# Experts' gate and up projections in three parts of 128 columns instead of four of 96

## The chip, the cores and the metric

The kernel runs on one core of one Trainium2 chip. The metric is the device time of one execution in microseconds (us). The core has a matrix engine (TensorE, PE in the profile; its weight loads have a row of their own, PEld), a vector engine (VectorE, DVE), a scalar engine (ScalarE, ACT), a general engine (GpSimd, POOL) and a sync engine (SyncE, SP) that issues most of the transfers. The 16 DMA engines of the core are shared by all queues. All data is fp32.

## The reference

The input is 16 sequences of 512 tokens with 256 features, 8192 tokens in all. Four layers follow one another, each with a layer norm ahead of it and a residual around it: a softmax attention, a mixture of experts, a forgetting linear attention, and the same mixture of experts again, with the same weights. Only the mixture of experts is touched here:

```python
logits = x @ router_w.T                          # 64 experts
topk_w, topk_ids = top_k(softmax(logits), 8)     # weights scaled to sum 1
# every expert takes at most C = 128 tokens, in order of the tokens
g = einsum('ecd,edf->ecf', xb, w_gate)           # 256 -> 192
u = einsum('ecd,edf->ecf', xb, w_up)             # 256 -> 192
h = silu(g) * u
y = einsum('ecf,efd->ecd', h, w_down)            # 192 -> 256
routed = sum over a token's experts of weight * y
gu = x @ ws_gate_up                              # shared expert, 256 -> 384
shared = silu(gu[:, :192]) * gu[:, 192:] @ ws_down
return routed + shared
```

## The kernel before

`hybrid_block_kernel` calls `attention`, `experts`, `forget_attention`, `experts` and `joined` in this order. `experts` (line 822) runs twice and has two phases, both ordered by hand on TensorE, VectorE, ScalarE and GpSimd (`manual_schedule`, line 1170): an engine executes in the order in which the code issues. The transfers that SP issues are placed among each other by a planner with its own costs, and SP takes them strictly in that order.

**Dense phase** (lines 1188 to 1203). It goes over 16 blocks of 512 tokens. In step `b` the code issues, in this order: `load(b+4)`, `normed(b+2)` (layer norm, line 97), `features(b+1)` (eight transposes of the normed block, line 910, and two copies by ScalarE, line 913), `shared(b-3)` (the shared expert's gate and up, line 989), `logits(b+1)` (line 919), `choose(b)` (the eight best experts, VectorE, lines 941 to 955), `likely(b+1)` (lines 931 to 936), `count(b-1)` (running counts of the tokens of each expert: a transpose, line 968, a copy, line 970, a scan, line 973, and two transfers through DRAM, lines 978 and 979), `down(b-4)` (the shared expert's down projection, line 1007, with copies at line 1014) and `moments(b+3)` (line 71). All PSUM results come from one pool of eight banks that are handed out in turn; one step takes two for `features`, four for `shared`, and one each for `logits`, `count` and two for `down`. A bank that is asked for waits until its last user eight banks earlier has been read.

**Shared expert.** `shared` (line 984) makes the 384 columns of gate and up in four parts of 96: two of gate, two of up, each in its own PSUM bank, 96 partitions x 512 tokens, with two matmuls over the 256 inputs. An fp32 matmul is two TensorE instructions in the profile, each with its own weight load, so a block has 16 at line 989. Then `gated` (line 813) is called twice. It computes silu(g) * u as 0.5 * (tanh(g/2) + 1) * g * u: one tanh on ScalarE (line 817) and two VectorE instructions (lines 818 and 819), the second waiting for the first.

**Expert loop** (lines 1204 to 1212). It goes over the 64 experts. In step `e`: `gather(e+6)` fetches the tokens of an expert by an indirect transfer that POOL issues (line 1108); a piece of `find` places the tokens of later experts (lines 1034 to 1083); `turned(e+2)` transposes the gathered tokens (line 1119) and copies them (VectorE, line 1121); `widened(e+1)` makes gate and up in four parts of 96 columns (line 1132: 16 TensorE instructions, 128 tokens each, all into one PSUM bank) and calls `gated` on 96 x 256 elements; `narrowed(e)` makes the down projection with two halves of 96 rows (line 1147: 4 instructions), scales it on ScalarE (line 1155) and adds it into DRAM by an indirect transfer that POOL issues (line 1158). Even and odd experts add into different tensors; a scatter into a tensor waits until the one before it into the same tensor has landed. `fetch` (line 1089) loads the weights of two experts with three transfers of 384 KB (gate, up, down) on SP; four such pairs fit (`p4`), so pair k+4 can be loaded when pair k has been used: the gate tile after line 1132 has read it, the down tile after line 1147 has.

Of the kernel before, what the change touches and what calls it, by code (L numbers as in the profile page):

```python
# [9 lines left out]
F32 = mybir.dt.float32  # L10
# [20 lines left out]
FP = 96  # L31
# [5 lines left out]
class Block:  # L37
# [775 lines left out]
    def gated(self, out, gate, up, pool, half):  # L813

        nc = self.nc
        th = pool.tile(list(out.shape), F32, name="th")
        nc.scalar.activation(th, gate, AF.Tanh, scale=0.5)  # L817
        nc.vector.scalar_tensor_tensor(th, th, 1.0, gate, ALU.add, ALU.mult)  # L818
        nc.vector.scalar_tensor_tensor(out, th, half, up, ALU.mult, ALU.mult)  # L819


    def experts(self, x, y, weights):
# [7 lines left out]
        with ExitStack() as c:  # L830
# [10 lines left out]
            nc.sync.dma_start(out=rw_sb, in_=rw.rearrange("(k p) f -> p k f", p=P))  # L841
            wsg_sb = w.tile([P, KD, 2 * FF], F32, name="wsg_sb")
            nc.sync.dma_start(out=wsg_sb, in_=ws_gu.rearrange("(k p) f -> p k f", p=P))
            wsd_sb = w.tile([FP, 2, D], F32, name="wsd_sb")
            nc.sync.dma_start(out=wsd_sb, in_=ws_down.rearrange("(k p) f -> p k f", p=FP))

# [32 lines left out]
            def bank():  # L879
                return pb.tile([P, BLK], F32, name="pb")  # L880
# [103 lines left out]
            def shared(b):  # L984
                xnT = xnTs.pop(b)
                gu = [bank() for m in range(4)]
                for m in range(4):
                    for kd in range(KD):
                        nc.tensor.matmul(  # L989
                            gu[m][0:FP, :],  # L990
                            lhsT=wsg_sb[:, kd, ts(m, FP)],
                            rhs=xnT[:, kd, :],
                            start=(kd == 0),
                            stop=(kd == KD - 1),
                        )
                hT = hTs[b] = p2.tile([FP, 2, BLK], F32, name="hT")
                for m in range(2):
                    self.gated(hT[:, m, :], gu[m][0:FP, :], gu[2 + m][0:FP, :], p2, 0.5)

            def down(b):  # L1000
                hT = hTs.pop(b)
                out = p2.tile([P, CB, D], F32, name="y")
                for i in range(0, CB, 2):
                    py = bank()
                    for k in range(2):
                        for m in range(2):
                            nc.tensor.matmul(
                                py[:, ts(k, D)],
                                lhsT=hT[:, m, ts(i + k, P)],
                                rhs=wsd_sb[:, m, :],  # L1010
                                start=(m == 0),
                                stop=(m == 1),
                            )
                    nc.scalar.copy(
                        out[:, i : i + 2, :], py.rearrange("p (c d) -> p c d", c=2)
                    )
                nc.sync.dma_start(
                    out=y[ts(b, BLK), :].rearrange("(c p) d -> p c d", p=P), in_=out
                )
# [66 lines left out]
            xes, xeTs, hes, ws = {}, {}, {}, {}  # L1086
            accs = (x, y)

            def fetch(e):

                es = slice(e, e + 2)
                wg = p4.tile([P, 2, KD, FF], F32, name="wg")
                nc.sync.dma_start(
                    out=wg, in_=w_gate[es].rearrange("e (p k) f -> p e k f", k=KD)
                )
                wu = p4.tile([P, 2, KD, FF], F32, name="wu")
                nc.sync.dma_start(
                    out=wu, in_=w_up[es].rearrange("e (p k) f -> p e k f", k=KD)
                )
                wd = p4.tile([FP, 2, 2, D], F32, name="wd")  # L1100
                nc.sync.dma_start(
                    out=wd, in_=w_down[es].rearrange("e (k p) f -> p e k f", p=FP)
                )
                ws[e // 2] = (wg, wu, wd)
# [19 lines left out]

            def widened(e):
                wg, wu, _ = ws[e // 2]
                xeT = xeTs.pop(e)
                gu = bank()[0:FP, :].rearrange("p (m t) -> p m t", m=4)
                for m in range(4):
                    wm = (wg, wu)[m // 2]  # L1130
                    for kd in range(KD):
                        nc.tensor.matmul(  # L1132
                            gu[:, m, :],
                            lhsT=wm[:, e % 2, kd, ts(m % 2, FP)],
# [4 lines left out]
                hes[e] = p3.tile([FP, 2, CAP], F32, name="he")  # L1139
                self.gated(hes[e], gu[:, 0:2, :], gu[:, 2:4, :], p3, 0.5)  # L1140

            def narrowed(e):
                wd = ws[e // 2][2]
                he = hes.pop(e)
                py = bank()
                for m in range(2):
                    nc.tensor.matmul(  # L1147
                        py[:, 0:D],
                        lhsT=he[:, m, :],
                        rhs=wd[:, e % 2, m, :],  # L1150
                        start=(m == 0),
                        stop=(m == 1),
                    )
# [16 lines left out]
            with tc.manual_schedule(  # L1170
# [34 lines left out]
                for e in range(-ahead, E):  # L1205
                    run(e + ahead, E, gather)
                    place((e + 14) // many * many, 1)
                    run(e + 2, E, turned)
                    run(e + 1, E, widened)
# [141 lines left out]
```

## Time and profile before

| | |
|---|---|
| three runs | 2975.1, 2981.86, 2982.6 us |
| median | 2981.86 us |
| the profiled execution | 2975.03 us, span 2972.9 us, mean granted TensorE clock 0.942 |
| attention | about 0 to 1299 us |
| first `experts`: dense phase, then expert loop | 1299 to 1598 us, 1598 to 1823 us |
| forgetting attention | about 1823 to 2376 us |
| second `experts` | 2376 to 2895 us |
| `joined` | to the end |

A window row gives for each engine its busy time and its number of instructions, then the granted clock of TensorE (1.00 is full speed), the share of the 16 DMA engines that was busy, and GB/s. A timeline row gives start, length, engine, line, operation, tiles and shapes; the square bracket gives the idle time of the engine before it and what ended it. Matmul lengths overlap: the spacing of their starts is what one costs. The stages' limits differ, so each is read from its own window.

### The profile page before, as it was taken

How to read it: one execution, taken by the hardware profiler on the slowest of the kernel's cores; microseconds unless marked ns; L12 is line 12 of the kernel's file. 1: busy time of each engine (PE TensorE's matmuls, PEld its weight loads, DVE VectorE, ACT ScalarE, POOL GpSimd, SP SyncE). 2: the span in 40 equal slices, each digit the busy share in tenths (PEclk: the TensorE clock that was granted, in tenths of full speed). 3: DMA queues.
4: the chain of work that ended last, by engine and by line, in shares of the span. 5: the costliest groups of instructions: out<-in, count | busy, mean ns of one | idle time of the engine just before them, and what ended most of it. 6: DMA issues, size and time to landing. Idle time of an engine off the chain costs nothing. (4 is left out here: it accounts for less than half of the span.)

```text
span 2972.9 us, 49634 instructions
## 1 busy us (share of the span) xinstructions
PE 2709.1 (91%) x19268; PEld 1667.1 (56%) x19268; DVE 1951.1 (66%) x4738; ACT 1153.6 (39%) x2227; POOL 724.9 (24%) x677
## 2 busy tenths in 40 slices
PE   7999999999999999978979995999999879979980
PEld 4444444444444444445648884576666655559870
DVE  5666666666666666537755553999999767736531
ACT  2555655555555565532221221434334212212220
POOL 2000000000000000001104776323322011117773
PEclk8999999999999999879989997999999969989995
DMA  1000000000000000045535996111110164339988
GB/s 44 1 16 16 16 16 16 15 9 8 16 16 16 16 16 8 8 134 135 141 88 158 249 251 156 35 47 53 53 40 27 29 198 133 108 81 246 249 192 339
DMA packets 216649, 252.15 MB, mean 85 GB/s; under 512 B 31712, under 2 KB 206432, under 8 KB 213344
## 3 DMA queue, kind: packets, MB, share of 16 engines
q1 hardware_dynamic: 190688, 202.83, 22.9%
q0 software_dynamic: 24576, 37.77, 6.5%
q10 hardware_dynamic: 1152, 8.39, 0.7%
q8 instruction: 153, 2.51, 0.3%
q14 instruction: 80, 0.66, 0.1%
HBM read 163.67 MB, written 84.74 MB: 84 GB/s over the span
## 5 line engine op out<-in xcount | busy, mean ns | idle before, releaser
L299 DVE TENSOR_REDUCE mx<-sc 128x1 f32<-128x512 f32 x1024 | 635.2, 682 | 395.2 <-PE sc L285 391.6
L326 ACT ACTIVATE pT<-sc 128x512 f32<-128x512 f32 x1024 | 528.7, 603 | 280.6 <-PE sc L285 280.4
L285 PE MATMUL sc<-kT,qT 16*128 16x512 f32 x2048 | 358.9, 611 | 1.4 <-DVE mx L299 1.4
L285 PE MATMUL sc<-qT,kT 17*128 17x512 f32 x2048 | 310.7, 647 | 0.0
L246 POOL TENSOR_TENSOR pad<-t,t 128x512 f32<-128x512 f32 x64 | 81.1, 1267 | 729.5 <-PE sc L285 577.7
L989 PE MATMUL pb<-xnT,wsg_sb 128*96 128x512 f32 x512 | 236.0, 608 | 18.2 <-DVE pr L933 18.2
L285 PEld LDWEIGHTS sc<-kT,qT 16*128 16x128 f32 x2048 | 167.6, 188 | 136.9 <-issue 58.5
L336 PE MATMUL sc<-pT,v 128*32 128x512 f32 x2048 | 241.4, 613 | 0.0
L687 DVE SCALAR_TENSOR_TENSOR pT<-sc,of,left 128x256 f32<-128x256 f32 x512 | 205.8, 473 | 10.3 <-PE sc L670 10.1
L817 ACT ACTIVATE th<-pb 96x256 f32<-96x256 f32 (+1 forms) x192 | 84.0, 453 | 305.5 <-PE pb L1132 266.0
L818 DVE SCALAR_TENSOR_TENSOR th<-th,pb 96x256 f32<-96x256 f32 (+1 forms) x192 | 96.7, 504 | 153.7 <-ACT th L817 152.2
L79 POOL TENSOR_SCALAR va<-mv 128x4 f32<-128x4 f32 x64 | 14.7, 229 | 680.3 <-DVE mv L73 456.4
L646 PE MATMUL pb<-feat,wqk_sb 128*128 128x512 f32 x384 | 176.6, 596 | 1.0 <-DVE left L629 1.0
L285 PEld LDWEIGHTS sc<-qT,kT 17*128 17x128 f32 x2048 | 89.9, 185 | 140.3 <-issue 103.9
L989 PEld LDWEIGHTS pb<-xnT,wsg_sb 128*96 128x96 f32 x512 | 82.5, 167 | 148.6 <-issue 105.2
L1108 POOL DMA_INDIRECT xe<-rows,token x128 | 133.1, 1040 | 111.5 <-DVE token L1082 73.1
L336 PEld LDWEIGHTS sc<-pT,v 128*32 128x32 f32 x2048 | 61.5, 112 | 173.1 <-issue 122.2
L219 PE MATMUL sc<-wqkv_sb,feat 128*128 128x512 f32 x256 | 135.2, 655 | 0.1
L936 ACT ACTIVATE pr<-pr 128x256 f32<-128x256 f32 x32 | 13.3, 417 | 312.5 <-DVE pr L933 308.2
L1132 PE MATMUL pb<-xeT,wg 128*96 128x128 f32 x1024 | 132.9, 273 | 0.4 <-DVE xeT L1121 0.4
L1147 PE MATMUL pb<-wd,he 96*128 96x256 f32 x512 | 131.9, 379 | 1.2 <-DVE he L819 1.2
L1132 PE MATMUL pb<-xeT,wu 128*96 128x128 f32 x1024 | 132.7, 273 | 0.0
(156 smaller groups left out, 4626.2 us busy)
## 6 DMA issues: line engine op xcount, KB each, us to landing
wg<-in_w_gate SPq DMA_DIRECT2D x64, 384.0 KB
wu<-in_w_up SPq DMA_DIRECT2D x64, 384.0 KB
wd<-in_w_down SPq DMA_DIRECT2D x64, 384.0 KB
rows<-xn SPq DMA_DIRECT2D x32, 512.0 KB
routed<-y SPq DMA_DIRECT2D x32, 512.0 KB
x<-in_x SPq DMA_DIRECT2D x16, 512.0 KB
attended<-x SPq DMA_DIRECT2D x16, 512.0 KB
x<-attended SPq DMA_DIRECT2D x16, 512.0 KB
```

The source lines that it names most:

```text
L219: nc.tensor.matmul(pq, lhsT=xnTs[b][:, kd, ts(i, P)], rhs=wqkv_sb[:, kd, 0 : 2 * D], start=(kd == 0), stop=(kd == KD - 1),)
L285: nc.tensor.matmul(scs[j], lhsT=lhs[at : at + high, ts(i, P)], rhs=rhs[at : at + high, :], start=True, stop=True,)
L299: nc.vector.tensor_reduce(mxs[n][:, i, j : j + 1], sc, AX.X, ALU.max, negate=True)
L326: nc.scalar.activation(pT[:, j, :], sc, AF.Exp, scale=float(HD) ** -0.5)
L336: nc.tensor.matmul(pav[ts(j, HP), :], lhsT=vs[b % 2][:, i, 4 * hg + j, :], rhs=pT[:, j, :], start=(i == 0), stop=(i == CB - 1),)
L646: nc.tensor.matmul(pq, lhsT=wqk_sb[:, kd, ts(m, P)], rhs=xnTs[b][:, kd, :], start=(kd == 0), stop=(kd == KD - 1),)
L687: nc.vector.scalar_tensor_tensor(pTs[n][:, :, ts(s8, HD)], sc[:, :, ts(s8, HD)], of[:, s8 : s8 + 1], here, ALU.mult, ALU.mult,)
L818: nc.vector.scalar_tensor_tensor(th, th, 1.0, gate, ALU.add, ALU.mult)
L989: nc.tensor.matmul(gu[m][0:FP, :], lhsT=wsg_sb[:, kd, ts(m, FP)], rhs=xnT[:, kd, :], start=(kd == 0), stop=(kd == KD - 1),)
L1108: nc.gpsimd.indirect_dma_start(out=xes[e], out_offset=None, in_=rows, in_offset=bass.IndirectOffsetOnAxis(ap=token[:, e : e + 1], axis=0),)
L1132: nc.tensor.matmul(gu[:, m, :], lhsT=wm[:, e % 2, kd, ts(m % 2, FP)], rhs=xeT[:, kd, :], start=(kd == 0), stop=(kd == KD - 1),)
L1147: nc.tensor.matmul(py[:, 0:D], lhsT=he[:, m, :], rhs=wd[:, e % 2, m, :], start=(m == 0), stop=(m == 1),)
```

## The change

The 192 + 192 columns of gate and up are cut into three parts of 128 instead of four of 96: the first 128 columns of gate, the first 128 of up, and a part that holds the last 64 of gate on partitions 0 to 63 and the last 64 of up on partitions 64 to 127. This applies to the shared expert and to the 64 experts.

For the shared expert the combined part is made when its weights are loaded: the one transfer of `ws_gate_up` becomes three column ranges, and that of `ws_down` becomes two row ranges (128 and 64). For the 64 experts gate and up of a pair share one tile, `wide`, loaded by two transfers as before, and a new ScalarE copy, `joined`, puts the two times 64 columns of one expert side by side in a tile `wc`, one expert earlier than `widened` uses it. `w_down` of a pair is loaded by two transfers, of 128 and of 64 rows. The down projection uses 128 and 64 rows.

`gated` is gone. The tanh and the first VectorE instruction go over 128 partitions, up columns included, whose results are not used; the last multiplication is two VectorE instructions, the second of 64 partitions with its PSUM operand read from partitions 64 to 127. In `shared` the two first VectorE instructions come ahead of the two last ones.

```diff
-FP = 96
+FT = FF - P
...
             wsg_sb = w.tile([P, KD, 2 * FF], F32, name="wsg_sb")
-            nc.sync.dma_start(out=wsg_sb, in_=ws_gu.rearrange("(k p) f -> p k f", p=P))
-            wsd_sb = w.tile([FP, 2, D], F32, name="wsd_sb")
-            nc.sync.dma_start(out=wsd_sb, in_=ws_down.rearrange("(k p) f -> p k f", p=FP))
+            for to, of, n in ((0, 0, FF), (FF, FF + P, FT), (2 * P, FF, P)):
+                nc.sync.dma_start(
+                    out=wsg_sb[:, :, to : to + n],
+                    in_=ws_gu[:, of : of + n].rearrange("(k p) f -> p k f", p=P),
+                )
+            wsd_sb = w.tile([P, 2, D], F32, name="wsd_sb")
+            nc.sync.dma_start(out=wsd_sb[:, 0, :], in_=ws_down[0:P, :])
+            nc.sync.dma_start(out=wsd_sb[0:FT, 1, :], in_=ws_down[P:FF, :])
...
             def shared(b):
                 xnT = xnTs.pop(b)
-                gu = [bank() for m in range(4)]
-                for m in range(4):
+                gu = [bank() for m in range(3)]
+                for m in range(3):
                     for kd in range(KD):
                         nc.tensor.matmul(
-                            gu[m][0:FP, :],
-                            lhsT=wsg_sb[:, kd, ts(m, FP)],
+                            gu[m],
+                            lhsT=wsg_sb[:, kd, ts(m, P)],
...
-                hT = hTs[b] = p2.tile([FP, 2, BLK], F32, name="hT")
+                hT = hTs[b] = p2.tile([P, 2, BLK], F32, name="hT")
+                th = p2.tile([P, 2, BLK], F32, name="th")
                 for m in range(2):
-                    self.gated(hT[:, m, :], gu[m][0:FP, :], gu[2 + m][0:FP, :], p2, 0.5)
+                    nc.scalar.activation(th[:, m], gu[m], AF.Tanh, scale=0.5)
+                    nc.vector.scalar_tensor_tensor(
+                        th[:, m], th[:, m], 1.0, gu[m], ALU.add, ALU.mult
+                    )
+                for o, g, u in (
+                    (hT[:, 0], th[:, 0], gu[2]),
+                    (hT[0:FT, 1], th[0:FT, 1], gu[1][FT:P]),
+                ):
+                    nc.vector.scalar_tensor_tensor(o, g, 0.5, u, ALU.mult, ALU.mult)
...
             def fetch(e):
...
+                wide = p4.tile([P, 2, 2, KD, FF], F32, name="wide")
+                for u, wt in enumerate((w_gate, w_up)):
+                    nc.sync.dma_start(
+                        out=wide[:, :, u], in_=wt[es].rearrange("e (p k) f -> p e k f", k=KD)
+                    )
+                wd = p4.tile([P, 2, 2, D], F32, name="wd")
+                for m, rs in enumerate((slice(0, P), slice(P, FF))):
+                    nc.sync.dma_start(
+                        out=wd[0 : rs.stop - rs.start, :, m, :],
+                        in_=w_down[es, rs].rearrange("e p f -> p e f"),
+                    )
+                ws[e // 2] = (wide, wd)
...
+            def joined(e):
+
+                wc = wcs[e] = p3.tile([P, KD, 2, FT], F32, name="wc")
+                nc.scalar.copy(
+                    wc, ws[e // 2][0][:, e % 2, :, :, P:FF].rearrange("p u k f -> p k u f")
+                )
+
             def widened(e):
-                wg, wu, _ = ws[e // 2]
+                wide = ws[e // 2][0][:, e % 2]
+                wc = wcs.pop(e).rearrange("p k u f -> p k (u f)")
+                parts = (wide[:, 0, :, 0:P], wc, wide[:, 1, :, 0:P])
                 xeT = xeTs.pop(e)
-                gu = bank()[0:FP, :].rearrange("p (m t) -> p m t", m=4)
-                for m in range(4):
-                    wm = (wg, wu)[m // 2]
+                gu = bank()[:, 0 : 3 * CAP].rearrange("p (m t) -> p m t", m=3)
+                for m, part in enumerate(parts):
                     for kd in range(KD):
                         nc.tensor.matmul(
                             gu[:, m, :],
-                            lhsT=wm[:, e % 2, kd, ts(m % 2, FP)],
+                            lhsT=part[:, kd, :],
                             rhs=xeT[:, kd, :],
...
-                hes[e] = p3.tile([FP, 2, CAP], F32, name="he")
-                self.gated(hes[e], gu[:, 0:2, :], gu[:, 2:4, :], p3, 0.5)
+                he = hes[e] = p3.tile([P, 2, CAP], F32, name="he")
+                th = p3.tile([P, 2, CAP], F32, name="th")
+                nc.scalar.activation(th, gu[:, 0:2, :], AF.Tanh, scale=0.5)
+                nc.vector.scalar_tensor_tensor(th, th, 1.0, gu[:, 0:2, :], ALU.add, ALU.mult)
+                for o, g, u in (
+                    (he[:, 0], th[:, 0], gu[:, 2, :]),
+                    (he[0:FT, 1], th[0:FT, 1], gu[FT:P, 1, :]),
+                ):
+                    nc.vector.scalar_tensor_tensor(o, g, 0.5, u, ALU.mult, ALU.mult)
...
                     run(e + 2, E, turned)
+                    run(e + 2, E, joined)
                     run(e + 1, E, widened)
                     run(e, E, narrowed)
```

More of the change, by code (lines that the diff above doesn't have):

```diff
@@ L811, in forget_attention @@
                         run(b + far, self.nblk, work, *args)
[L813 to L819, printed above, removed]
     def experts(self, x, y, weights):
@@ L1005, in down @@
                     for k in range(2):
-                        for m in range(2):
+                        for m, high in enumerate((P, FT)):
                             nc.tensor.matmul(
                                 py[:, ts(k, D)],
-                                lhsT=hT[:, m, ts(i + k, P)],
-                                rhs=wsd_sb[:, m, :],
+                                lhsT=hT[0:high, m, ts(i + k, P)],
+                                rhs=wsd_sb[0:high, m, :],
                                 start=(m == 0),
@@ L1083, in find @@
                 yield
-            xes, xeTs, hes, ws = {}, {}, {}, {}
+            xes, xeTs, hes, ws, wcs = {}, {}, {}, {}, {}
             accs = (x, y)
@@ L1091, in fetch @@
                 es = slice(e, e + 2)
[L1092 to L1104, printed above, removed]
+                wide = p4.tile([P, 2, 2, KD, FF], F32, name="wide")
[10 more added lines that the diff above has]
+                ws[e // 2] = (wide, wd)
             def gather(e):
@@ L1138, in widened @@
                         )
-                hes[e] = p3.tile([FP, 2, CAP], F32, name="he")
-                self.gated(hes[e], gu[:, 0:2, :], gu[:, 2:4, :], p3, 0.5)
+                he = hes[e] = p3.tile([P, 2, CAP], F32, name="he")
[7 more added lines that the diff above has]
+                    nc.vector.scalar_tensor_tensor(o, g, 0.5, u, ALU.mult, ALU.mult)
             def narrowed(e):
-                wd = ws[e // 2][2]
+                wd = ws[e // 2][1]
                 he = hes.pop(e)
                 py = bank()
-                for m in range(2):
+                for m, high in enumerate((P, FT)):
                     nc.tensor.matmul(
                         py[:, 0:D],
-                        lhsT=he[:, m, :],
-                        rhs=wd[:, e % 2, m, :],
+                        lhsT=he[0:high, m, :],
+                        rhs=wd[0:high, e % 2, m, :],
                         start=(m == 0),
```

## The prediction

> **What bounds the kernel now.** The page comes first: TensorE is busy for 91% of the span.
>
> ```profile
> span 2972.9 us, 49634 instructions
> PE 2709.1 (91%) x19268; PEld 1667.1 (56%) x19268; DVE 1951.1 (66%) x4738; ACT 1153.6 (39%) x2227; POOL 724.9 (24%) x677
> ```
>
> That is a mean over stages. The change lives in the two passes of `experts`, so I read the timeline of one steady block of the dense phase.
>
> ```profile
> 1452.36 3.64 PE L989 MATMUL pb<-xnT,wsg_sb 128*96 128x512 f32 x8 [0.85 <-DVE pr L933]
> ...
> 1457.55 0.16 DVE L88 SCALAR_TENSOR_TENSOR t<-y 128x4 f32<-128x4 f32 x1 [1.47 <-POOL y L81]
> ...
> 1459.43 0.68 DVE L818 SCALAR_TENSOR_TENSOR th<-th,pb 96x512 f32<-96x512 f32 x1
> 1460.21 0.68 DVE L819 SCALAR_TENSOR_TENSOR hT<-th,pb 96x512 f32<-96x512 f32 x1
> 1460.82 0.68 DVE L818 SCALAR_TENSOR_TENSOR th<-th,pb 96x512 f32<-96x512 f32 x1
> ...
> 1466.22 0.42 DVE L933 TENSOR_TENSOR pr<-pb,mx 128x256 f32<-128x256 f32 x1
> 1466.79 3.65 PE L989 MATMUL pb<-xnT,wsg_sb 128*96 128x512 f32 x8 [0.86 <-DVE pr L933]
> ```
>
> The period is 14.43 us (1452.36 to 1466.79). TensorE waits 0.86 us of it, for a PSUM bank that line 933 must first read. VectorE has no such slack: its only gaps are 1.0 us (the scan waits for ScalarE's copy) and 1.47 us (line 88 waits for POOL), both inside its own chain from 933 to 933. So the steady dense block is paced by VectorE, with TensorE 0.86 us behind.
>
> Next, the expert loop by windows and its queues (the second fence is the DMA view from 1600 to 1800 us).
>
> ```profile
> 1620.00:1640.00 20.00, 20.00 (x159) 19.09 (x158) 13.55 (x30) 5.35 (x13) 15.46 (x13) 1.00 0.93 254
> 1680.00:1700.00 20.00, 18.13 (x140) 16.75 (x139) 12.41 (x26) 5.13 (x12) 14.45 (x11) 1.00 1.01 266
> 1800.00:1820.00 20.00, 17.42 (x130) 15.90 (x128) 6.51 (x17) 5.60 (x13) 14.83 (x11) 1.00 0.51 74
> 1598.00:1820.00 222.00, 209.75 (x1598) 195.26 (x1598) 118.50 (x262) 54.70 (x128) 159.37 (x119) 1.00 0.90 228
> ```
>
> ```profile
> q1 hardware_dynamic: 26432, 33.04, 55.2%
> q0 software_dynamic: 10343, 15.89, 39.4%
> ```
>
> TensorE is busy 210 of 222 us; the DMA engines reach a share of 1.0 in the windows in which TensorE pauses. POOL has a pace of its own: gather 0.99 us, scatter 1.59 us and 0.30 us ahead of each make 3.18 us per expert. So three resources stand close together: TensorE 210 us, DMA about 200 us (the eleven 20-us shares from 1600 sum to 10.01), POOL 196 us (64 scatters x 1.89 + 58 gathers x 1.29).
>
> **The change part by part.**
>
> *TensorE in the loop.* Spacing is needed, and whether 128-column weights keep it:
>
> ```profile
> 1730.67 0.93 PEld L1132 LDWEIGHTS pb<-xeT,wu 128*96 128x96 f32 x8
> 1731.55 0.73 PEld L1147 LDWEIGHTS pb<-wd,he 96*128 96x128 f32 x4
> ...
> 1461.46 1.04 PE L910 MATMUL pb<-ident,xn 128*128 128x128 f32 x8
> 1462.34 1.02 PE L989 MATMUL pb<-xnT,wsg_sb 128*96 128x512 f32 x2
> ```
>
> Eight instructions of line 1132 take 0.88 us, 0.110 each. Eight transposes with 128 columns of weights and 128 of data also take 0.88 us, 0.110 each. So 12 instead of 16 instructions save 4 x 0.110 = 0.44 us per expert, 28 us per loop of TensorE time. Bounds: nothing hidden would be 0.108 (line 919: 128-column loads, 16 in 1.73 us) + 0.110 = 0.218 each, 12 x 0.218 = 2.62 against 1.76 us, 0.86 us per expert slower; I take 0.110, since the transposes have the same two sizes.
>
> The Trainium skill speaks against this: TensorE: Matmul & The Clock Gate, LDWEIGHTS, prices a weight load by its columns, about columns / 1.2 ns, that is 80 ns for 96 and 107 ns for 128. By it 16 x 80 and 12 x 107 are the same 1.28 us, and a loop paced by weight loads would gain nothing; the trace has both sizes at the same 0.110 us.
>
> *What then bounds the loop.* TensorE's 210 us become about 182; DMA's 200 and POOL's 196 stay and are the next late ones. Today the last down weights of the loop are issued at 1795.21 us, and the last copy scaled at line 1155 is at 1818.10: TensorE trails. With TensorE off the bound, the DMA engines can stay at a share near 1.0, from 0.963 on average between 1620 and 1800 (180 us: 173.6 us of work, 6.6 us won), and the last experts follow their weights sooner (the last window has a share of 0.51; some 4 to 8 us won). I take 10 us per loop. Ends: 0 if POOL and DMA are the bound already; 15 if everything closes up to 207 us.
>
> *ScalarE in the loop.* The new copy has 256 elements per partition from SBUF: line 936, 128x256, is 0.417 us. ScalarE does 5 of 20 us there and idles 1.45 to 3.5 us ahead of each tanh, so it costs nothing; uncovered it would be 128 x 0.42 = 54 us. The wait it adds is for the weights of expert e+2; behind it in ScalarE's queue stand the tanh of e+1 and the scaling of e, and behind that POOL's scatter. Pairs are issued some 20 us ahead of use, a gather lands in 4.9 us, so I cost the wait at nothing while the cushion holds, and as the weights fall behind at 0.4 us per pair at most.
>
> *VectorE in the loop.* One 96x256 (0.416 us) becomes two of 128 elements. Between 0.162 us (line 594, 16 elements) and 0.416 us (256), 128 elements are 0.28 us; 2 x 0.28 - 0.416 = +0.15 us per expert. VectorE is busy 11 to 13 of 20 us, he(e+1) is needed 2.5 us after its matmuls end and takes 1.35: hidden. Uncovered, 19 us in both loops.
>
> *Weights' transfers.* Gate and up keep their 1536-byte rows. Down keeps 384 rows of 1 KB per pair, in two transfers: one more SP issue (0.33 us) per pair, 32 per loop; SP waits for buffers there, not the buffers for SP. The nearest row for a packet is q1's mean, 55.2% x 200 x 16 / 26432 = 67 ns. If the 128 packets onto 64 partitions took twice that, a pair would cost 128 x 67 / 16 = 0.54 us more, 15 us per loop; if the same, nothing. I take nothing and keep 15 as the end.
>
> SBUF — State Buffer, Door 1: The DMA port swizzle, is the second rule against: partitions 0 to 63 reach only half of the SBUF ports, and one transfer over 128 partitions is preferred. By it the 96-row tile put 256 of 384 KB through those ports, and the new pair puts 128 + 128 KB: the same load, so the sum would be zero by the rule too. No row here shows ports.
>
> *Dense phase, steady.* Line 989 falls from 16 to 12 instructions of 0.435 us (7.03 / 16): 1.74 us per block of TensorE, off the path, because VectorE sets the period. VectorE keeps four instructions of 512 elements. But the order changes: 818 to 819 (dependent) are 0.78 us apart, 819 to 818 (not) 0.61. With both first ones ahead, all four stand 0.61 apart: 2 x 0.17 = 0.34 us per block, over the 10 or so blocks of steady state 3.4 us per pass (ends 0 and 4.5). Banks: nine per step in place of ten; the third part still waits for 933.
>
> *Dense phase, blocks that TensorE paces.* The first two and the last two of a pass have 16 of line 989 in one go, and VectorE waits for their last parts (0.80 and 2.12 us ahead of 819 at 1524.54 and 1535.30). Up to 4 x 1.74 us; but VectorE, and then SP's wait for the transfers of the counts, take most of it. I take 2.5 us, ends 0 and 7.
>
> *From dense phase to loop.* From 1566.59 to 1593.7 TensorE runs without a gap two blocks of `shared` and three of `down`, the gathers having been issued by 1577.8. So 2 x 1.74 = 3.5 us go straight off the path (ends 2 and 3.5; the next late one is the gathers).
>
> *Start of a pass.* SP issues three more transfers (0.46 us each) ahead of `load`, and the shared weights come in 768 rows of 768, 512 and 256 bytes in place of 256: 512 x 67 / 16 = 2.1 us. Against that SP idles 1.6 us for the last store. I charge 1 us, ends 0 and 3.5.
>
> **Sum.** Per pass 10 + 3.4 + 2.5 + 3.5 - 1 = 18.4 us; two passes 36.8. The profiled execution took 2975.03 us (span 2972.9 plus 2.1 around it), so 2938; it was the shortest of what is shown, 6.8 us under the median of 2981.86. I go half the way: 2942 us.
>
> **The rivals.**
>
> *Dense only.* POOL and DMA already pace the loop: it gains nothing. For it: scatter and gather with their 0.30 us gaps make 3.18 of the 3.47 us per expert, and scatters land after some 5.4 us with two experts to a tensor. Against: whole windows have TensorE at 20 of 20. Two passes x 8.4 = 17 us: 2962 on the same footing.
>
> *All of TensorE's time counts.* The loops win 2 x 20 and the dense phase 2 x 10: 2975 - 60, with half of 6.8 back: 2918. Against: DMA's 200 us.
>
> *Nothing in the sum.* The two halves of the down weights cost DMA 8 to 10 us more per loop and eat the rest: 2975 to 2985.
>
> *Slower: ScalarE's new wait idles POOL.* If weights arrive late, `joined` holds the scaling of e, and POOL's scatter with it. POOL has 6.36 us of work per pair of experts and 6.94 us in which to do it. A stall over 0.58 us per pair makes the loop longer; over 0.85 it eats the dense gain too. At 1.5 us, (6.36 + 1.5) x 32 = 251 against 222 us: +29 - 8 per pass, 3017 us. Against: the cushion of 20 us. The same end would come from weight loads that are not hidden (+0.86 us per expert).
>
> **How the numbers follow.** The forecast with both gains 0.47, dense only 0.18, all of TensorE's time 0.10, nothing 0.10, slower 0.15. A change within 0.3% (about 9 us) is what a measurement of this kernel can't tell from none. Faster: 0.47 + 0.18 + 0.10 = 0.75; same 0.10; slower 0.15. The forecast's own range is 2925 to 2960; leaving out a tenth at each side, with the ends of the unknown costs, gives 2915 to 2988.
>
> **What would show it.** Right: 12 instructions of line 989's successor per block at 0.435 us and a dense period near 14.1 us with longer waits of TensorE; 12 per expert in the loop at 0.110 us; a loop of about 212 us with the DMA share near 1.0 from start to end and TensorE waiting for weights or gathers. Wrong: spacing over 0.13 us with 128 columns; POOL idle behind line 1155; a DMA share of 1.0 with fewer GB/s than 250; a later first load at the start of a pass.

## The result, and the profile after

The changed kernel takes 2986.0 us (median of 10 runs) where the kernel before took 2978.9 (10 runs on the same chip): the ratio is 1.0029, with a 95% interval of 1.0018 to 1.0041. On a second chip it was 1.0036 (1.0023 to 1.0049). The change costs some 7 to 11 us; the forecast was a gain of 37. The profiled execution has a span of 2984.3 us against 2972.9.

The head of the page of the changed kernel:

```profile
span 2984.3 us, 48565 instructions
...
PE 2708.4 (91%) x18628; PEld 1576.8 (53%) x18628; DVE 1987.8 (67%) x4866; ACT 1191.6 (40%) x2355; POOL 729.6 (24%) x677
```

TensorE executes 640 instructions fewer and is busy as long as before (2709.1 us). So something else got longer. The groups by form, first of the kernel before (down projection of the loop, then of the dense phase), then of the changed kernel; the last two numbers ahead of the idle time are the busy total and the mean ns of one:

```profile
L1147 PE MATMUL pb<-wd,he 96*128 96x256 f32 x512 | 131.9, 379 | 1.2 <-DVE he L819 1.2
L1007 PE MATMUL pb<-wsd_sb,hT 96*128 96x256 f32 x512 | 116.9, 382 | 0.0
```

```profile
L1014 PE MATMUL pb<-wsd_sb,hT 64*128 64x256 f32 x256 | 91.2, 437 | 0.0
L1168 PE MATMUL pb<-wd,he 64*128 64x256 f32 x256 | 89.3, 429 | 0.0
L1014 PE MATMUL pb<-wsd_sb,hT 128*128 128x256 f32 x256 | 88.4, 428 | 0.0
...
L1168 PE MATMUL pb<-wd,he 128*128 128x256 f32 x256 | 77.5, 385 | 0.6 <-DVE he L1161 0.6
```

The down projection has as many instructions as before, but 179.6 us of busy time in the dense phase in place of 116.9, and 166.8 in the loop in place of 131.9. The weight loads say why. This is the timeline of a dense block, weight loads alone, first of the kernel before, then of the changed one; the brackets hold the idle time ahead of a group:

```profile
1457.90 3.32 PEld L1007 LDWEIGHTS pb<-wsd_sb,hT 96*128 96x128 f32 x16
```

```profile
1486.28 0.44 PEld L966 LDWEIGHTS pb<-ident,chosen 128*64 128x64 f32 x4
1486.72 0.30 PEld L1014 LDWEIGHTS pb<-wsd_sb,hT 128*128 128x128 f32 x2
1487.35 0.29 PEld L1014 LDWEIGHTS pb<-wsd_sb,hT 64*128 64x128 f32 x2 [0.33 <-issue]
1487.97 0.30 PEld L1014 LDWEIGHTS pb<-wsd_sb,hT 128*128 128x128 f32 x2 [0.33 <-issue]
```

Each change between a matmul over 128 rows and one over 64 leaves the weight loads idle for 0.33 us; the sixteen loads over 96 rows follow one another without such a gap, and so do the loads behind line 966, which has 64 columns but 128 rows. A matmul is two instructions here, so a block's 16 have eight such changes, the last of them into the transposes that follow. TensorE's timeline at the same places:

```profile
1458.01 3.62 PE L1007 MATMUL pb<-wsd_sb,hT 96*128 96x256 f32 x16
```

```profile
1486.82 4.99 PE L1014 MATMUL pb<-wsd_sb,hT 128*128 128x256 f32 x16
1491.74 1.09 PE L908 MATMUL pb<-ident,xn 128*128 128x128 f32 x8
```

From start to start the sixteen take 4.92 us (1486.82 to 1491.74), where line 1007 took 3.45 (1458.01 to 1461.46): 0.18 us per change.

An expert of the loop on TensorE, before (first fence) and after; line 1119, now 1125, are the two transposes:

```profile
1645.56 1.03 PE L1147 MATMUL pb<-wd,he 96*128 96x256 f32 x4
1646.42 0.39 PE L1119 MATMUL pb<-ident,xe 128*128 128x128 f32 x2
1646.65 1.04 PE L1132 MATMUL pb<-xeT,wg 128*96 128x128 f32 x8
...
1648.40 1.03 PE L1147 MATMUL pb<-wd,he 96*128 96x256 f32 x4
```

```profile
1734.63 0.51 PE L1125 MATMUL pb<-ident,xe 128*128 128x128 f32 x2
1734.97 0.61 PE L1146 MATMUL pb<-xeT,wide 128*128 128x128 f32 x4
...
1736.31 1.22 PE L1168 MATMUL pb<-wd,he 128*128 128x256 f32 x4
1737.47 0.51 PE L1125 MATMUL pb<-ident,xe 128*128 128x128 f32 x2
```

Before, start to start: 0.23 us for the transposes, 1.75 for gate and up, 0.86 for down, 2.84 in all. After: 0.34, 1.34 and 1.16, again 2.84. Gate and up run at 0.11 us per instruction with 128 columns, so that step of the forecast holds and 0.41 us are saved; the two changes of height, into the 64 rows and out of them, take 0.41 us back, 0.2 each.

The dense block and the loop, by the views that the prediction used:

```profile
1481.40 0.42 DVE L931 TENSOR_TENSOR pr<-pb,mx 128x256 f32<-128x256 f32 x1
...
1484.29 2.26 PE L917 MATMUL pb<-rw_sb,xnT 128*128 128x64 f32 x16 [0.37 <-ACT xnT L911]
...
1489.05 1.27 DVE L998 SCALAR_TENSOR_TENSOR th<-th,pb 128x512 f32<-128x512 f32 x2
1490.25 1.40 DVE L1005 SCALAR_TENSOR_TENSOR hT<-th,pb 128x512 f32<-128x512 f32 x2
...
1495.72 0.42 DVE L931 TENSOR_TENSOR pr<-pb,mx 128x256 f32<-128x256 f32 x1
```

```profile
1620.00:1640.00 20.00, 20.00 (x133) 15.95 (x133) 15.19 (x38) 7.67 (x20) 14.62 (x12) 1.00 0.98 263
1680.00:1700.00 20.00, 18.83 (x126) 14.90 (x125) 13.44 (x33) 6.90 (x18) 16.12 (x12) 1.00 1.02 264
...
1800.00:1820.00 20.00, 14.16 (x85) 10.07 (x83) 6.27 (x18) 5.64 (x14) 12.95 (x9) 0.88 0.64 117
```

The block's period is 14.32 us (14.43 before) and VectorE still sets it. In the loop the DMA share (last but one) averages 0.98 between 1620 and 1780 us, against 0.96 before.

A third thing lies in a stage that the change doesn't touch, the forgetting attention behind the first loop. SP's issues and POOL's first addition there, of the changed kernel:

```profile
1814.52 0.37 SPq L464 DMA_DIRECT2D padded<-in_b_wqk  x1
1825.13 0.37 SPq L484 DMA_DIRECT2D gates_sb<-in_b_wf  x1
...
1828.02 0.65 SPq L553 DMA_DIRECT2D x<-attended  x1
...
1840.19 2.34 POOL L555 TENSOR_TENSOR x<-x,y 128x1024 f32<-128x1024 f32 x1 [5.80 <-DMA y<-routed]
```

Before, `padded` was asked for at 1586.90 us, in the dense phase, and three loads of x at 1823.97, ahead of `gates_sb` at 1826.48. Now `padded`, 1 MB, goes out in the last microseconds of the loop and every x behind the weights.

The two passes by stages. "Maxima" is the first instruction that writes `mx`, "find" the first of `lies`, "copy" the last scaled `ye`:

| us | before, pass 1 / 2 | after, pass 1 / 2 | forecast |
|---|---|---|---|
| router weights issued to first maxima | 20.8 / 21.0 | 21.8 / 20.7 | +1 |
| first to last maxima (steady blocks) | 199.9 / 200.2 | 198.6 / 198.5 | -3.4 |
| last maxima to find | 36.3 / 36.4 | 36.3 / 36.5 | -2.5 |
| find to first scatter | 47.8 / 46.7 | 48.2 / 49.2 | -3.5 |
| first scatter to last copy (loop) | 214.3 / 211.0 | 209.9 / 212.6 | -10 |
| last copy to first addition, line 555 | 19.4 / - | 25.7 / - | 0 |

### The profile page after: what moved, and what is told of

Same layout as the page of the kernel before. It is cut to its first block, busy times and chain, and to the rows that moved or that the text cites. A ratio compares the mean times of both kernels' runs of the same rounds, so it can differ in the third digit from the quotient of the medians.

```text
span 2984.3 us, 48565 instructions
## 1 busy us (share of the span) xinstructions
PE 2708.4 (91%) x18628; PEld 1576.8 (53%) x18628; DVE 1987.8 (67%) x4866; ACT 1191.6 (40%) x2355; POOL 729.6 (24%) x677
## 4 chain that ended last, share of the span: by engine, by line
PE 72%; DVE 13%; DMA 8%; POOL 3%; issue 2%; ACT 2%; SPq 1%; POOLq 0%; ACTq 0%; DVEq 0%
PE sc L285 19%; PE sc L336 8%; PE sc L219 5%; PE pb L1146 4%; PE pb L646 3%; PE pb L1014 3%; PE pb L1168 3%; DMA xe<-rows,token 3%; PE pb L987 2%; DVE pT L687 2%; PE sc L272 2%; PE sc L308 2%; PE sc L252 2%; PE sc L359 2%; PE pb L744 2%
## 5 line engine op out<-in xcount | busy, mean ns | idle before, releaser
L285 PEld LDWEIGHTS sc<-kT,qT 16*128 16x128 f32 x2048 | 166.8, 188 | 137.1 <-issue 58.5
L987 PE MATMUL pb<-xnT,wsg_sb 128*128 128x512 f32 x384 | 182.4, 620 | 1.3 <-DVE pr L931 1.0
L1014 PE MATMUL pb<-wsd_sb,hT 128*128 128x256 f32 (+1 forms) x512 | 163.8, 432 | 0.0
L1146 PE MATMUL pb<-xeT,wide 128*128 128x128 f32 x1024 | 159.2, 279 | 0.7 <-DVE xeT L1127 0.5
L1168 PE MATMUL pb<-wd,he 128*128 128x256 f32 (+1 forms) x512 | 157.8, 407 | 0.6 <-DVE he L1161 0.6
L1146 PEld LDWEIGHTS pb<-xeT,wide 128*128 128x128 f32 x1024 | 138.6, 196 | 1.7 <-DVE xeT L1127 1.1
L1155 ACT ACTIVATE th<-pb 128x256 f32<-128x256 f32 x128 | 49.1, 384 | 207.5 <-PE pb L1146 193.6
L654 ACT ACTIVATE ez<-pb,bqk_sb 128x512 f32<-128x512 f32 x96 | 66.0, 687 | 140.9 <-PE pb L646 140.1
```

The lines of the kernel that those rows point to most:

```text
L285: nc.tensor.matmul(scs[j], lhsT=lhs[at : at + high, ts(i, P)], rhs=rhs[at : at + high, :], start=True, stop=True,)
L987: nc.tensor.matmul(gu[m], lhsT=wsg_sb[:, kd, ts(m, P)], rhs=xnT[:, kd, :], start=(kd == 0), stop=(kd == KD - 1),)
L1014: nc.tensor.matmul(py[:, ts(k, D)], lhsT=hT[0:high, m, ts(i + k, P)], rhs=wsd_sb[0:high, m, :], start=(m == 0), stop=(m == 1),)
L1146: nc.tensor.matmul(gu[:, m, :], lhsT=part[:, kd, :], rhs=xeT[:, kd, :], start=(kd == 0), stop=(kd == KD - 1),)
L1168: nc.tensor.matmul(py[:, 0:D], lhsT=he[0:high, m, :], rhs=wd[0:high, e % 2, m, :], start=(m == 0), stop=(m == 1),)
```

## The experiments

Theory A: the change of height costs about 0.19 us of TensorE and eats the gain. Theory L: the changed kernel takes 7 KB more SBUF per partition in `experts` (`th` of the dense phase 8 KB in place of 4, `wc` 3 KB), so that tiles of the next stage come to lie on memory that the loop uses to its end, and their loads wait. Against them: TensorE's time is worth little in the loop; the clock or scatter explains the later stage.

**e1: heights of 96 and 64 in the kernel before.**

```diff
-                                lhsT=hT[:, m, ts(i + k, P)],
-                                rhs=wsd_sb[:, m, :],
+                                lhsT=hT[0 : (FP, 64)[m], m, ts(i + k, P)],
+                                rhs=wsd_sb[0 : (FP, 64)[m], m, :],
...
-                        lhsT=he[:, m, :],
-                        rhs=wd[:, e % 2, m, :],
+                        lhsT=he[0 : (FP, 64)[m], m, :],
+                        rhs=wd[0 : (FP, 64)[m], e % 2, m, :],
```

> The kernel before, with nothing changed but the rows of the down projection's second half: 64 in place of 96, in the dense phase and in the expert loop (32 of 192 rows of the gated product are left out of the sum, so the output differs; the number of instructions is the same). Theory A (a change between a full-height and a 64-row matmul costs TensorE about 0.19 us, 0.37 us per expert and 1.5 us per dense block, and TensorE is what the loop waits for): four down instructions of two experts take 1.26 us in place of 0.89, weight loads of line 1147 stand behind idle of 0.33 us, TensorE gets 24 us more work per loop, and the loop of 214 us becomes 228 to 238; a dense block gets 1.5 us more of TensorE against 0.86 us of idle. In all 40 to 65 us slower than before. Rival B (the loop is paced by POOL and the DMA engines, TensorE's time is worth little): the loop grows by less than 8 us, in all under 20 us. Rival C (64 rows cost nothing by themselves; the changed kernel's down projection is slow for another reason, such as its 128-row weights): within 5 us of before.

Measured: 3013.1 us against 2975.7, ratio 1.0115 (1.0099 to 1.0131): 37 us slower from fewer rows alone, a little under the 40 that Theory A named as its least. The four down instructions take 1.16 us from start to start, 0.86 before. Rival C falls: 64 rows beside 96 behave as 64 beside 128, and 96 beside 128 cost nothing in the kernel before. But the 37 us lie elsewhere than Theory A had them: the loops grew by 8 and 11 us (to 222.1 each), not by 14 to 24; the steady period stayed at 14.43 us; the two stretches from the last maxima to the first scatter grew from 84.0 to 97.2 and from 83.2 to 92.9. That is where the dense phase pays: TensorE now needs 14.88 us per steady block, falls behind VectorE's 14.43 block by block, and catches up at the end. (By an estimate from the granted clock some 5 of the 13 us in the first pass go with a lower one, 0.77 from `find` to the first scatter against 0.83 before.) The windows of its loop:

```profile
1680.00:1700.00 20.00, 20.00 (x140) 16.28 (x139) 11.23 (x25) 4.74 (x12) 15.05 (x12) 1.00 1.00 252
1800.00:1820.00 20.00, 20.00 (x139) 16.02 (x138) 7.73 (x19) 5.12 (x12) 14.10 (x11) 1.00 1.03 272
```

Here TensorE waits 0.4 us in the whole loop, so its 222 us are what TensorE needs. Of the 64 experts 12 have a piece of `find` behind them, whose 64-row matmuls brought both changes already before; for the other 52 two changes at 0.2 us are new, 21 us. Without them TensorE needs about 201 us, an estimate from these rows. It says what the prediction misread: its 210 us of busy time were counted from 1598 to 1820 us, a window that reaches beyond the loop at both ends. From the first scatter to the last copy TensorE was busy for 204.2 us in the kernel before, 3 more than its need, and the two loops took 214.3 and 211.0: some 10 to 13 us of each were no work of TensorE's.

**e2: 7 KB more SBUF in the kernel before.** The same instructions; two tiles are allocated larger than they are used.

```diff
-        th = pool.tile(list(out.shape), F32, name="th")
+        if len(out.shape) == 2:
+            th = pool.tile([FP, 2, BLK], F32, name="th")[:, 0, :]
+        else:
+            th = pool.tile(list(out.shape), F32, name="th")
...
-                hes[e] = p3.tile([FP, 2, CAP], F32, name="he")
+                hes[e] = p3.tile([FP, 4, CAP], F32, name="he")[:, 0:2, :]
```

> The kernel before, with the same instructions, but 7 KB more SBUF per partition in experts (two tiles made larger than what is used of them), as the changed kernel takes. Theory L (the larger footprint moves the tiles of the next stage onto memory that the loop uses to its end, so that the forgetting attention's first loads are issued after its weights and everything in that stage is later): the first addition at line 555 comes about 4 us later after the last scatter, the forgetting attention takes 9.6 us more (549.2 to 559 us), in all 8 to 10 us slower. Rival (the 9.6 us come from the clock, or from noise between executions): no change, within 3 us.

Measured: 2983.6 us against 2975.7, ratio 1.0023 (1.0013 to 1.0034): 7.9 us for memory that nobody reads. SP and POOL execute the forgetting attention in the same order as in the changed kernel. First the line of the kernel before, then e2:

```profile
1823.97 1.96 SPq L553 DMA_DIRECT2D x<-attended  x3
```

```profile
1823.38 0.37 SPq L464 DMA_DIRECT2D padded<-in_b_wqk  x1
1834.73 0.37 SPq L484 DMA_DIRECT2D gates_sb<-in_b_wf  x1
...
1837.62 0.67 SPq L553 DMA_DIRECT2D x<-attended  x1
...
1849.19 2.34 POOL L555 TENSOR_TENSOR x<-x,y 128x1024 f32<-128x1024 f32 x1 [5.23 <-DMA y<-routed]
```

From the last copy to the first addition it takes 25.8 us, as in the changed kernel (25.7), against 19.4. Theory L is right in its place and its total, wrong in its sum: the forgetting attention as the expectation counts it (from the issue of `gates_sb` to the next pass) took 551.0 us, not 559. Some 3 us lie ahead of it, where the last scatters and the 1 MB of `padded` are under way together. What SP waits for ahead of `padded` points to whose memory it takes: in the kernel before and in e3 the shared expert's gate and up (lines 989 and 987), in the changed kernel and in e2 the down projection of the loop (lines 1168 and 1150), for 18.8 and 17.8 us.

**e3: the changed kernel with the old footprint.**

```diff
-                th = p2.tile([P, 2, BLK], F32, name="th")
+                th = [p2.tile([P, BLK], F32, name="th") for m in range(2)]
...
-                wc = wcs[e] = p3.tile([P, KD, 2, FT], F32, name="wc")
+                wc = wcs[e] = p2.tile([P, KD, 2, FT], F32, name="wc")
...
-                he = hes[e] = p3.tile([P, 2, CAP], F32, name="he")
-                th = p3.tile([P, 2, CAP], F32, name="th")
+                he = hes[e] = p2.tile([P, 2, CAP], F32, name="he")
+                th = p2.tile([P, 2, CAP], F32, name="the")
```

> The changed kernel with the footprint of the one before: the tanh tiles of the dense phase are two of 512 elements as before, and the copied columns, th and he of the loop have two buffers in place of three. Theory L: the forgetting attention returns from 558.7 to about 549 us, and the time falls by 7 to 10 us, to 2976 to 2979. Rival (clock or noise): 2986 as before, within 3 us. If a third buffer was needed in the loop, it gets longer than 210 us.

Measured: 2979.5 us, ratio 1.0016 (1.0004 to 1.0028). The order of SP and POOL is that of the kernel before again, x goes out three at a time at 1823.72 us, and last copy to first addition takes 21.0 us. The loops (212.4 and 212.8) don't miss the third buffers. The ratio alone doesn't settle it, since its interval touches that of the changed kernel; the places in the trace, and e2, do.

**e4: 128 rows in the second half too.** The rows past 64 are zeros, written once per pass into tiles that stay in place.

```diff
+            nc.gpsimd.memset(wsd_sb[FT:P, 1, :], 0.0)
+            hT2 = [w.tile([P, 2, BLK], F32, name=f"hT{i}") for i in range(2)]
+            for t in hT2:
+                nc.gpsimd.memset(t[FT:P, 1, :], 0.0)
...
-                hT = hTs[b] = p2.tile([P, 2, BLK], F32, name="hT")
+                hT = hTs[b] = hT2[b % 2]
...
-                        for m, high in enumerate((P, FT)):
+                        for m, high in enumerate((P, P)):
```

`he` and `wd` of the loop get the same treatment; the rest is e3.

> As the last one, and the down projection's second half is multiplied over all 128 rows, 64 of them zeros that are written once per pass (tiles that stay in place). Theory A: four down instructions of two experts take 0.89 us in place of 1.26, sixteen of a dense block 3.5 in place of 5.0; the loop loses 5 to 10 us, the dense phase and what follows 5 us per pass; 2945 to 2960 in all, 20 to 30 us faster than before. Rival B (POOL and DMA pace the loop): only the dense part comes, 2965 to 2970. Rival C (the height of the matmul is not the cause): same as the last one, 2976 to 2979.

Measured: 2957.7 us against e3's 2979.5 and the 2975.7 of before, all on one chip; ratio to before 0.9937 (0.9923 to 0.9951). More rows of work, 22 us less time than e3: Theory A's sign and its total hold. TensorE's busy total falls to 2634.6 us. The stretch from find to the first scatter in the changed kernel, then in e4 (TensorE's timeline):

```profile
1575.26 4.99 PE L1014 MATMUL pb<-wsd_sb,hT 128*128 128x256 f32 x16
...
1585.43 10.01 PE L1014 MATMUL pb<-wsd_sb,hT 128*128 128x256 f32 x32
```

```profile
1571.67 3.62 PE L1024 MATMUL pb<-wsd_sb,hT 128*128 128x256 f32 x16
...
1575.12 5.31 PE L997 MATMUL pb<-xnT,wsg_sb 128*128 128x512 f32 x12
1580.27 7.07 PE L1024 MATMUL pb<-wsd_sb,hT 128*128 128x256 f32 x32
```

(A group carries the shape of its first instruction; in the changed kernel every second pair has 64 rows.) Find to first scatter is 43.7 and 43.8 us, last maxima to find 30.1 and 35.5. Against e3 the two stretches from the last maxima to the first scatter give 17 us. The loops, 209.6 and 209.8, give 3 each where 5 to 10 were expected: most of the gain lies ahead of the loop. The clock doesn't explain it: from find to the first scatter e3 was granted 0.83 and 0.81, e4 0.81 in both passes. Some 5 of the 17 us, in the first pass alone, also hang on the order of SP's queue (e11).

**e5: without most of the weights' transfers.**

```diff
             def fetch(e):
 
+                if e >= 8:
+                    ws[e // 2] = ws[e // 2 - 4]
+                    return
```

> The kernel of e4 with the weights of only the first eight experts loaded; the other 56 compute with these again (so the output differs), and some 44 MB per pass aren't moved. Theory D (with the row changes gone, the DMA engines pace the loop: their share was 0.97, and TensorE waited 47 us of 180 for gathers): the loop from the first scatter to the last scaled copy falls from 209.7 us to the pace of POOL, 196 to 203 us, and TensorE's waits for xe shrink. Theory T (TensorE or the chain through ScalarE and VectorE paces it still): 207 to 210 us, unchanged.

Measured: 2927.1 us (ratio 0.9835, 0.981 to 0.9861), loops of 197.8 and 196.6 us.

```profile
1680.00:1700.00 20.00, 18.55 (x137) 17.10 (x136) 13.41 (x35) 7.24 (x20) 16.11 (x13) 1.00 0.52 90
```

With the DMA share at half, the loop falls by 12 to 13 us to the 196 that the prediction gave for POOL. Theory D holds in that the weights' transfers set e4's loop. One part of it failed: between 1620 and 1780 us the matmuls still wait 11.8 us for gathers, against 16.7 in e4; POOL, now the pace, issues them. (The 47 us of the expectation add the waits of the weight loads and of the matmuls for the same gathers; the matmuls alone waited 19.5 us of the 180.)

**e6, e7, e9: the parts apart.** e6 is e4 with 64 rows in the loop again; e7 has e4's dense phase with the loop of before; e9 the dense phase of before with e4's loop.

```diff
@@ e6, narrowed
-                for m, high in enumerate((P, P)):
+                for m, high in enumerate((P, FT)):
```

> The kernel of e4 with 64 rows back in the expert loop alone; the dense phase keeps 128. Theory D (the loop waits for DMA more than for TensorE): the 24 us that the row changes put on TensorE per loop show as 3 us (212.5 against 209.7), 2961 to 2966 in all. Theory T (TensorE paces the loop): 10 us or more per loop, 2978 or above.

> The dense phase of e4 (three parts of 128, down over 128 rows) with the expert loop of before (four parts of 96, down over 96 and 96, no copied columns). If the loop's part of the change is worth what the prediction said (10 us per pass), 2975 to 2980; if it is worth what e4's loops show (before's were 214.3 and 211.0, e4's 209.6 and 209.8 us: 4.8 and 1.2), 2962 to 2966.

> The counterpart of e7: the dense phase of before (four parts of 96, down over 96 and 96) with the expert loop of e4 (three parts of 128, copied columns, down over 128 rows with 64 zeros). If the loop's part is worth the 10 us per pass of the prediction, 2953 to 2960; by the loops of e4 and e7 (209.7 against 216.4 and 211 to 214) it is worth 2 to 5 us per pass, 2965 to 2973. If the parts add up, the gains of e7 (11 us) and of this run make together the 18 to 22 us of e4 and e6.

Measured:

| | time, before beside it | ratio (95%) | loops |
|---|---|---|---|
| e6 | 2953.4, 2975.8 | 0.9922 (0.9905 to 0.9939) | 208.4, 214.2 |
| e7 | 2964.7, 2975.8 | 0.9960 (0.9944 to 0.9975) | 216.4, 216.4 |
| e9 | 2971.9, 2978.0 | 0.9980 (0.9968 to 0.9991) | 211.4, 212.8 |

In the loop the change of height costs nothing that these runs can tell: e6 is not slower than e4. The dense part is worth 11 us, the loop's part 6 (3 to 10 by e9's interval), together 17 against the 18 to 22 of the whole: they add up. One loop's length scatters by some 3 us between executions, in part with the granted clock (0.98 in e7's loops of 216.4 us, 1.00 in before's two). The means agree with e9: four parts of 96 (before, e2, e7) 213.8 us over six loops, three of 128 with full rows (e4, e9) 210.9 over four. The loop's part is worth some 3 us per pass; with 64 rows (the changed kernel, e3, e6, e8, e10, e11) twelve loops average 212.2 us.

**e8: the second token group's halves in turned order**, from e3.

```diff
-                        for m, high in enumerate((P, FT)):
+                        for m in (k, 1 - k):
+                            high = (P, FT)[m]
...
-                                start=(m == 0),
-                                stop=(m == 1),
+                                start=(m == k),
+                                stop=(m != k),
```

> The kernel of e3 (128 and 64 rows everywhere, small footprint), with the order of the two halves turned for every second token group of the dense phase, so that two 64-row matmuls follow each other: eight changes of height in place of sixteen per block. Theory A (price per change, about 0.19 us with two to a pair): sixteen down instructions of a block take about 4.25 us in place of 5.0, and half of the dense gain of e4 comes: from find to the first scatter 46 in place of 48.6 us, in all 2969 to 2975. If the price belongs to the 64-row matmul and not to the change, 5.0 us and 2979 as in e3.

(The expectation counts each change twice; counted in matmuls they fall from eight per block to four.) Measured: 2974.6 us against 2975.8, ratio 0.9995 (0.9984 to 1.0005).

```profile
1577.03 4.40 PE L1015 MATMUL pb<-wsd_sb,hT 128*128 128x256 f32 x16
...
1586.42 8.64 PE L1015 MATMUL pb<-wsd_sb,hT 128*128 128x256 f32 x32
```

By these lengths sixteen instructions take 3.62, 4.40 and 4.99 us (e4, e8, the changed kernel) with none, four and seven changes inside the group, the eighth lying behind it; 32 take 7.07, 8.64 and 10.01 with none, eight and fifteen. That is 0.195 to 0.196 us per change in all four cases. The price belongs to the change and not to the 64 rows, which are as many in e8 as in the changed kernel. The 46 us from find to first scatter didn't come (48.0 and 49.0): the granted clock from find to the first scatter was 0.78 and 0.77, against 0.83 and 0.81 in e3. In the first pass, behind the last `down`, it was 0.54 to 0.60 from 1597 to 1605 us, where `find`'s matmuls of line 1059 then took 0.77 us per pair in place of 0.46. Why the clock fell there and not in e3 is open.

**e10: the changed kernel again**, unaltered, beside e9.

> The changed kernel itself, beside e9 on the same chip. Its first run had 543.7 us from the first addition of the forgetting attention to the next pass, where six other kernels, one of them with the same order of instructions in that stage, had 533.6 to 536.5. If that was one execution's scatter, it is 533 to 540 now, and the 25.7 us from the last scaled copy to that addition stay (the layout); if it belongs to the changed kernel, 543 us again. Time 1.001 to 1.005 of before.

Measured: 2988.2 us against 2978.0, ratio 1.0036 (1.0023 to 1.0049). Last copy to first addition: 25.4 us, so the layout's share is there again. From there to the next pass 539.3 us this time, 541.5 in e9 (which has the early order), 533.6 to 538.2 in the others: the 543.7 of the first trace was mostly that execution's, and what is left isn't tied to the change.

**e11: weights asked for earlier**, from e6. In e6 the last maxima are at 1521.79 us in the first pass and at 2577.85 in the second. SP's queue behind them:

```profile
1537.61 0.45 SPq L986 DMA_DIRECT2D counts<-cum  x1
1540.65 2.08 SPq L987 DMA_DIRECT2D cw<-counts  x2
```

```profile
2591.44 0.55 SPq L1111 DMA_DIRECT2D wide<-in_w_up  x1
2597.61 0.27 SPq L987 DMA_DIRECT2D cw<-counts  x1
2597.93 1.12 SPq L1116 DMA_DIRECT2D wd<-in_w_down  x2
2599.15 0.55 SPq L986 DMA_DIRECT2D counts<-cum  x1
```

In the first pass the last `counts` go out 15.8 us after the last maxima, in the second 21.3, behind a transfer of `wide`, a `cw` that waits 5.5 us for the counts before it, and two of `wd`.

```diff
-                    if nb - 4 <= b < nb:
-                        fetch(2 * (b - nb + 4))
+                    if nb - 6 <= b < nb - 2:
+                        fetch(2 * (b - nb + 6))
```

> The kernel of e6, with the first four pairs of weights asked for two steps earlier in the dense phase. In e6's first pass the last counts are issued 15.8 us after the last choice of maxima and find begins 30.0 us after it; in its second pass two weight transfers and a wait for the counts before stand ahead on SP, and the numbers are 21.3 and 35.2. If that queue is the cause, find begins 30 us after it in both passes, 5 us less in all: 2945 to 2951. If something else makes the second pass later, 2950 to 2957 as before. If the earlier transfers get in the way of the dense phase's loads, its steady period rises over 14.32 us.

Measured: find begins 29.9 and 29.6 us after the last maxima, so the queue was the cause of the second pass's 5 us; the steady blocks keep their 198.6 us. 2952.1 us against 2979.4, ratio 0.9914 (0.9900 to 0.9927). Its interval overlaps that of e6, so only the stage shows the 5 us. This version beats both kernels: 27 us under before. What the earlier request alone would bring to the kernel before was not run.

## Why the prediction was wrong, step by step

The forecast gained 36.8 us against the profiled execution; the change lost 7, so some 44 were missed. The runs split them: 22 from e3 to e4 for the height changes (5 of them through SP's order in one pass), 4 to 8 for the layout (by e3 and by e2), and the 19 by which e4, with both costs gone, still falls short of the forecast, about 14 of them in the loops and 4 in the steady blocks. The parts come from different chips and agree with the 44 within their noise.

*The step that failed first* is the change "part by part" itself: the down projection's new shape, 128 and 64 rows in place of 96 and 96, was noted for its transfers and never for its matmuls. It got no term, not even bounds. The sum took it at nothing; it cost 0.195 us per change, eight changes per dense block and two per expert, and without them e4 is 22 us faster than e3. The row stood in the trace of before: ahead of the first 64-row load of `find`, behind a 96-row matmul, line 1051 shows the same idle 0.33 us, and the down projection over 96 rows shows none.

```profile
1648.29 0.73 PEld L1147 LDWEIGHTS pb<-wd,he 96*128 96x128 f32 x4
1649.35 0.29 PEld L1051 LDWEIGHTS pb<-cw,lies 64*128 64x128 f32 x2 [0.33 <-issue]
```

The Trainium skill has a rule that bears on it: TensorEngine Tiling (Array Packing), Tiling Modes, says under Key Properties that changing the tiling mode drains TensorE, and lists 64 by 128 under Available Configurations, beside 128 by 128. It states no price, and not whether a plain matmul over 64 rows counts as such a mode. The idle 0.33 us fit a drain; no run here tells it from another cause.

*TensorE in the loop.* 0.110 us with 128 columns is right. The 0.41 us saved per expert were spent again on two height changes; but by e6 this hardly mattered.

*What then bounds the loop* was mis-sized: 10 us per pass taken, some 3 measured with full rows. The step took TensorE's 210 us of busy time in a window of 222 for what holds the loop, where the need is about 201 (e1) in loops of 211 to 214 us; and it took the DMA engines' 0.963 share for slack that could be closed, but the share was already about what it is afterwards (0.97 to 0.98 between 1620 and 1780 us in e4 and the changed kernel). The weights' transfers hold e4's loop at 209 us, with POOL at 196 behind them (e5). For the kernel before this was not run; its matmuls too waited for gathers, 8.1 us between 1620 and 1800. Of the rivals, "dense only" described the loop best, and its 2962 is near e4's 2957.7; it lacked the two costs. "Nothing in the sum" comes near the measured time, but by a cost of the down weights that didn't come: that is luck.

*Dense phase, steady.* The order gain on VectorE came (four instructions in 2.5 us in place of 2.8), but 0.1 of it was lost ahead of line 929: 14.43 to 14.32, 1.5 us per pass in place of 3.4.

*Blocks that TensorE paces* and *from dense phase to loop*: 2.5 and 3.5 were taken, nothing came. On the way into the loop eight changes cost 1.47 us per block of the 1.74 that the shorter line 987 saves; with full rows this term was right (47.2 to 43.8 us on average). Ahead of it SP's queue sets the pace: the last `counts` went out 22 us after the last maxima (21.3 and 21.5 us in the kernel before), and find followed some 14 us later. With full rows that term was 1 to 6, the larger value where the counts go ahead on SP. *Start of a pass*: 1 us was charged, +1.0 and -0.3 came.

*Costed at nothing and right*: the copy on ScalarE, its new wait (POOL waited 4.0 us in all for `wc` between 1620 and 1800), and the down weights in two transfers: 33.04 MB took 51.9% of the 16 engines between 1600 and 1800 us, 55.2% before. The rival of a stalled POOL didn't come, so the kernel got slower for other reasons than the text had ready. *Not thought of*: that more SBUF in one stage moves the loads of the next. And a change of 0.3%, which the forecast held for unmeasurable, was told from none: the interval of ten runs is 0.12% to either side.

## What to carry to other kernels

When a matmul's contraction is split, look at the heights of neighbours on TensorE: 96 with 96 or 128 cost nothing here, 64 beside either cost about 0.2 us per change, and padding 64 rows with zeros to 128 was cheaper than leaving them out. A larger tile in one stage can delay the first loads of the next, so compare where each queue issues those loads, not only the stage that was edited. Before taking an engine's busy time for its need, find a stretch in which it has no gap, count by the spacing there, and set it against a time with the same start and end.

## What was not expected of the hardware

A matmul over fewer rows can make a kernel slower: in e1, 64 rows in place of 96 cost 37 us. The weight loads stop overlapping for 0.33 us at each change of height, in either direction, and the price of a change came out at 0.195 us with four per block and with eight.
